# An output product on TensorE: four plain tile products against seven products of half blocks

## The chip, the cores and the metric

The kernel runs on one core of one Trainium2 chip. The metric is the device time of one execution in microseconds (us); where several executions were timed, their median is given.

## The reference, cut to what matters

Two transformer layers run one after the other over 4 sequences of 512 tokens, 512 features wide, all in float32. The first layer adds to its input an attention with 16 heads of 128 features (a sparse part over compressed entries, top 8 of them, and a local window part) and a mixture of experts. The end of that attention is the product in question:

```
merged = (ctx_sparse + ctx_local) * 0.5
out = merged.transpose(0, 2, 1, 3).reshape(Bq, Sq, NH * D) @ Wo + bo
...
x = x + _L0_attn_ref(xn, ...) + _L0_ffn_ref(xn, ...)
```

`merged` has 2048 features (16 heads of 128), and `Wo` takes them to 512. The second layer, an attention with 16 heads of 32 features and another mixture of experts, is not touched.

## The kernel before, in words

Layer 0's attention is cut into 32 steps. A step (index `i`) takes one group `g` of two heads and one sequence `b` of 512 tokens; `b` runs fastest, so that a group's weights serve four steps. Here is what one step does, with the line numbers of the profile:

- `project(i + 1)` makes the queries, keys and values of the *next* step (line 675 records all its matmuls, tile `p`). It already works with seven products of half blocks: `first`, `second`, `third`, `fourth` and `fifth` hold the products p1 to p7, VectorE (DVE) adds their results (lines 710 to 739), and rotates them (lines 585 to 588). `combine_weights` (line 119) makes the sums of weights that it needs, once a group.
- `scores` multiplies this step's queries with compressed keys (`sp`, line 758) and with the window's keys (`st`, line 767). DVE then picks the top 8 of the compressed scores (lines 761 to 783), ScalarE (ACT) takes exponentials (lines 771 and 784), and GpSimd (POOL) multiplies the window's weights with a mask (`lT`, line 775).
- `context` makes the weighted sums of values (lines 809 to 827), for each of the two heads.
- `turn_context` transposes a head's context on TensorE (PE), and ACT copies it to the tile `cT` (lines 834 and 835), which holds [128 features, 2 heads, 512 tokens].
- `output(i, t, cT)`, for the four tiles `t` of 128 tokens, multiplies `cT` with the group's two blocks of `Wo`, adds both heads in one PSUM bank (line 842), and DVE adds the bank to the running sum `acc` (line 845). `acc` holds all 2048 tokens by 512 features in SBUF and becomes the input of the next layer.

PSUM has eight banks: three for the tag `mm` (the products p, `op`, and the experts' products), three for `sc` (scores and contexts), two for `tr` (transposes). A product that wants an `mm` bank waits until DVE has read what stands in it.

Jobs of the rest of the layer are put at fixed places between (`run0((i, place))`): normalising and compressing of sequences in steps 0 to 4, routing in steps 3 and 4, the experts (`hp_r`, line 529, `yr_r`, line 532) from step 5 on, adding their results to `acc` (line 852) from about step 24 on, the first norms of layer 1 in steps 29 to 31. The weights `Wo` of a group are loaded by `load_out` (line 109) into a single buffer at the group's first step, once the last step of the group before has used them. SyncE's queue (SP) issues most transfers; POOL issues the gathers of the experts (lines 481 and 545), whose descriptors go to a scratch in SBUF.

Each engine works through its own queue in order. A scheduler in the framework decides the order in a queue, beginning from the program's order; engines wait for each other by semaphores.

Of the kernel before, what the change touches and what calls it, by code (L numbers as in the profile page):

```python
# [12 lines left out]
F32 = mybir.dt.float32  # L13
I32 = mybir.dt.int32
AF = mybir.ActivationFunctionType
ALU = mybir.AluOpType
# [4 lines left out]
P = 128  # L21
B, S, HID = 4, 512, 512
T = B * S
NT = T // P
TC = S // P
# [24 lines left out]
def two_layers(ctx: ExitStack, tc: tile.TileContext, a: dict, out: bass.AP, large: bass.AP):  # L50
# [3 lines left out]
    nc = tc.nc  # L54
    V, G, A, PE = nc.vector, nc.gpsimd, nc.scalar, nc.tensor
# [8 lines left out]
    wpool = layer0.enter_context(tc.tile_pool(name="wattn", bufs=2))  # L64
    const0 = layer0.enter_context(tc.tile_pool(name="const0", bufs=1))
    qp = layer0.enter_context(tc.tile_pool(name="qkv", bufs=2))
# [6 lines left out]
    def psum(tag, name):  # L73
        return ps.tile([P, 512], F32, tag=tag, name=name, bufs={"mm": 3, "sc": 3, "tr": 2}[tag])

    def load(pool, name, shape, src):
        t = pool.tile(shape, F32, tag=name, name=name, bufs=1)
        nc.sync.dma_start(out=t, in_=src)
        return t
# [8 lines left out]
    def load_block(g, nm, between=None):  # L88


        w = wpool.tile([P, KC, 3 * D], F32, tag=nm, name=f"{nm}_{g}", bufs=1 if nm == "wA" else 2)
        for f in range(2):
            nc.sync.dma_start(out=w[:, ts(f, 2), :],
                              in_=a[nm][g, ts(f, 2 * P), :].rearrange("(k p) c -> p k c", p=P))
            if between:
                between(nm, f)
        return w

    def load_later(g):

        w = load_block(g, "wB")
        b2 = wpool.tile([P, 2, 3 * D], F32, tag="b2", name=f"b2_{g}")
        for i, nm in enumerate(("bA", "bB")):
            nc.sync.dma_start(out=b2[:, i, :], in_=a[nm][g].partition_broadcast(P))
        return [[None, w], b2]

    def load_out(g):
        wo = wpool.tile([P, HG, HID], F32, tag="Wo", name=f"Wo_{g}", bufs=1)
        nc.sync.dma_start(out=wo, in_=a["Wo"][ds(g * HG * D, HG * D), :].rearrange("(h p) c -> p h c", p=P))
        return wo  # L110
# [11 lines left out]
            tc.keep_in_program_order(d)  # L122
        sums_w[g] = t2_, t3_, t4_

    sums_w, out_w = {}, {}
    wk = wv = bkv = cmask = lmask = eidx = row = part = None


    acc = keep.tile([P, NT, HID], F32, tag="acc", name="acc")
# [8 lines left out]
    def load_x(n):  # L138
        nc.sync.dma_start(out=acc[:, n, :], in_=x_v[:, n, :])
# [61 lines left out]
    def tables():  # L201

        for hs, w in ((0, 0), (1, 0), (2, 1)):
            tc.keep_in_program_order(G.tensor_tensor(t1[:, :, hs, :], cos[:, 0:TC], own_(w, TC, 0, R), ALU.mult))
            for half, other in ((0, 1), (1, 0)):
                tc.keep_in_program_order(G.tensor_tensor(t2[:, :, hs, ts(half, 32)], sin[:, 0:TC, ts(half, 32)], own_(w, TC, 32 * other, 32), ALU.mult))
# [252 lines left out]
    class Experts:  # L459
# [53 lines left out]
        def turn(self, i):  # L513
            x = self.x[i]
            tr = self.bank("tr", f"trm_{self.r.name}_{i}")
            for k in range(KC):
                PE.transpose(tr[:, ts(k, P)], x[:, ts(k, P)], ident)  # L517
            xT = self.pool.tile([P, KC, P], F32, tag="xT", name=f"xT_{self.r.name}_{i}")
            A.copy(xT, tr.rearrange("p (k t) -> p k t", k=KC))  # L519
            self.x[i] = xT  # L520
# [117 lines left out]
    steps = [(g, b) for g in range(NH // HG) for b in range(B)]  # L638
# [4 lines left out]
    def load_sums(i):  # L643

        for n in range(4):
            xs[n] = wk0.tile([P, 2, 256], F32, tag=f"x{n}", name=f"x{n}_{i}", bufs=1)
            if i >= B:
                nc.sync.dma_start(out=xs[n].rearrange("p k t -> p (k t)"), in_=xsd[steps[i][1], n])
# [182 lines left out]
    def turn_context(i, h, ctx_, cT):  # L831
        tr = psum("tr", f"trc_{i}_{h}")
        for t in range(TC):
            PE.transpose(tr[:, ts(t, P)], ctx_[:, t, :], ident)
        A.copy(cT[:, h, :], tr)  # L835

    def output(i, t, cT):
        g, b = steps[i]
        wo = out_w[g]
        op = psum("mm", f"op_{g}_{b}_{t}")  # L840
        for h in range(HG):
            PE.matmul(op, lhsT=cT[:, h, ts(t, P)], rhs=wo[:, h, :],  # L842
                      start=(h == 0), stop=(h == HG - 1))
        n = b * TC + t
        V.tensor_tensor(acc[:, n, :], acc[:, n, :], op, ALU.add)  # L845

    def combine(ex, n):
        rs = ex.gather(n)

        def add():  # L850
            for k in range(2):
                tc.keep_in_program_order(V.scalar_tensor_tensor(
                    acc[:, n, :], rs[k], ex.r.gate[:, k, n : n + 1], acc[:, n, :], ALU.mult, ALU.add
                ))
        return add
# [29 lines left out]
    def start_sequence(n):  # L885
        for f in layernorm(n, sp0, psum, n >= TC):
            f()
# [4 lines left out]
    for b in range(1, B):  # L892
        i = b - 2
# [77 lines left out]
    for n in range(3 * TC):  # L971
        i, t = 29 + n // TC, n % TC
        last = t + 2 if t < 3 else 5
        if i + 1 == len(steps) and t == 3:
            last = 4
# [14 lines left out]
    def rest():  # L990
        nonlocal wk, wv, bkv, cmask, lmask, eidx, row, part
        start_sequence(2)
        start_sequence(3)
        tables()
        for n in range(TC, TC + 2):
            load_x(n)
        wk = load(sp0, "wk", [P, KC, D], a["Wk"].rearrange("(k p) d -> p k d", p=P))
        wv = load(sp0, "wv", [P, KC, D], a["Wv"].rearrange("(k p) d -> p k d", p=P))
        bkv = sp0.tile([P, 2, D], F32, tag="bkv", name="bkv", bufs=1)
        nc.sync.dma_start(out=bkv[:, 0, :], in_=a["bk"].partition_broadcast(P))  # L1000
        nc.sync.dma_start(out=bkv[:, 1, :], in_=a["bv"].partition_broadcast(P))
        for n in range(TC + 2, 2 * TC):
            load_x(n)
        out_w[0] = load_out(0)
        cmask = load(const0, "cmask", [P, SEEN[TC - 1].stop], a["c_cmask_seen"])
        lmask = load(const0, "lmask", [P, 2, 2, P], a["c_lmask01"])
        for n in range(2 * TC, NT):
            load_x(n)
        eidx = load(const, "eidx", [P, E], a["c_eidx"])
        row = load(const, "row", [P, P], a["c_row"])  # L1010
        part = load(const, "part", [P, 1], a["c_part"])
# [25 lines left out]
    for i, (g, b) in enumerate(steps):  # L1037
        if b == 0:
            if g:
                out_w[g] = load_out(g)  # L1040
            if g + 1 < NH // HG:
                groups[g + 1] = load_later(g + 1)
        more = i + 1 < len(steps)
        turn_last = turn_keys
        now = qkT
        cT = qp.tile([P, HG, S], F32, tag="cT", name=f"cT_{g}_{b}", bufs=1)
        nc.sync.dma_start(out=cv0s[i % 2][96:P, 0:D], in_=cv[0:32, b, 0:D])
        em0, lT0 = scores(i, 0, now)
        turn_last(1)
        if more:  # L1050
            load_sums(i + 1)
            qkT, sums_x, first, second, third, fourth, fifth, turn_queries, turn_keys = project(i + 1)
            first()
            sums_x()
            if b == 2 and g + 1 in groups:
                groups[g + 1][0][0] = load_block(g + 1, "wA")
        run0((i, 0))
        em1, lT1 = scores(i, 1, now)
        sT0 = turn(i, 0, em0)
        run0((i, 1))  # L1060
        if more:
            second(0)
            turn_queries(0)
        ctx0 = context(i, 0, lT0, sT0, lv)
        if more:
            second(1)
        sT1 = turn(i, 1, em1)
        if more:
            third()
        if b == 2 and g + 1 in groups:  # L1070
            combine_weights(g + 1)
        run0((i, 2))
        ctx1 = context(i, 1, lT1, sT1, lv)
        turn_context(i, 0, ctx0, cT)
        run0((i, 3))
        if more:
            fourth()


            if 5 <= i < 24:  # L1080
                turn_queries(1)
                turn_keys(0)
                fifth()
            else:
                fifth()
        turn_context(i, 1, ctx1, cT)
        if more and not 5 <= i < 24:
            turn_queries(1)
            turn_keys(0)
        run0((i, 3.5))  # L1090
        for t in range(TC):
            output(i, t, cT)
        run0((i, 4))
    scratch.close()
    layer0.close()
# [208 lines left out]
    left = {n: 2 for n in range(NT)}  # L1304
# [159 lines left out]
    for g in range(NG):  # L1464
        b, j = groups1[g]
# [32 lines left out]
    last = [psum1("st", f"o1_{n0 + t}", 2) for t in (0, 2)]  # L1498
    last = [last[t // 2][:, t % 2, :] for t in range(TC)]
# [709 lines left out]
```

## Time and profile before

| what | value |
| --- | --- |
| median of 3 runs | 2061.0 us (2060.38 to 2063.49) |
| profiled execution, its own time | 2062.1 us |
| its span in the profile | 2060.0 us |
| granted TensorE clock | 0.996 |
| PE busy | 2000.5 us, 9130 matmul records |
| DVE busy | 1450.3 us |
| ACT busy | 867.8 us |
| POOL busy | 750.8 us |
| matmuls of line 842 (output) | 512 records of 128x512, 229.0 us |
| adds of line 845 | 128 of 128x512, 87.4 us |

The profile shows each float32 matmul as two records, so that the 8 matmuls of a step's output product stand as 16 records. Durations of matmuls overlap (each is pipelined into the next); the pitch from one to the next is what counts. "Idle before" a group names what its engine waited for. Layer 0's steps lie between about 50 us and 1445 us of the span.

### The profile page before, as it was taken

The numbers are of one execution on the slowest core, as the hardware profiler recorded it, in microseconds if no ns is written. First come the engines' busy times: TensorE is split into PE (matmuls) and PEld (weight loads), VectorE is DVE, ScalarE is ACT, GpSimd is POOL, SyncE is SP. The second block draws the span as 40 slices with busy tenths as digits, with TensorE's granted clock in tenths as the row PEclk, the third lists the DMA queues.
The fourth block names the chain that finished last, engine by engine and source line by source line (L and its number), as shares of the span: only waits on it lengthen the run. The fifth ranks groups of instructions, "written<-read, shape, count | busy, mean of one in ns | idle before, by whom it ended". The sixth has DMA issues, their size and how long they took to land.

```text
span 2060.0 us, 27976 instructions
## 1 busy us (share of the span) xinstructions
PE 2000.5 (97%) x9130; PEld 1199.1 (58%) x9130; DVE 1450.3 (70%) x3543; ACT 867.8 (42%) x2600; POOL 750.8 (36%) x761
## 2 busy tenths in 40 slices
PE   7999999999999999999999999999999999999997
PEld 4666666666666666666666666666334445445442
DVE  7889967666766666676667787787595555557775
ACT  4554444344444443444444454454243432433332
POOL 4422244443323333334334444353114432432550
PEclk9999999999999999999999999999999999999999
DMA  7101133333332343244453222121317775773551
GB/s 251 68 34 60 42 125 133 125 108 113 125 132 101 110 154 103 93 136 162 179 182 113 72 82 75 51 73 62 120 36 260 255 253 200 261 251 119 154 165 51
DMA packets 98906, 267.23 MB, mean 130 GB/s; under 512 B 14400, under 2 KB 27840, under 8 KB 87488
## 3 DMA queue, kind: packets, MB, share of 16 engines
q0 software_dynamic: 27072, 148.91, 21.3%
q1 hardware_dynamic: 70528, 114.34, 16.5%
q10 hardware_dynamic: 1152, 2.10, 0.3%
q8 instruction: 75, 1.23, 0.2%
q14 instruction: 79, 0.65, 0.1%
HBM read 222.05 MB, written 42.73 MB: 129 GB/s over the span
## 4 chain that ended last, share of the span: by engine, by line
PE 80%; DVE 8%; POOL 3%; ACT 3%; issue 2%; DMA 2%; DVEq 0%; ACTq 0%; POOLq 0%
PE p L675 25%; PE hp_r L529 12%; PE op L842 11%; PE st L767 4%; PE sp L758 3%; PE st L1249 2%; PE cx L1263 2%; PE qp L1225 2%; PE ca L811 2%; DVE pS L1269 2%; PE o L1332 1%; PE trq L695 1%; PE trm_r L517 1%; PE trk L701 1%; PE cc L814 1%
## 5 line engine op out<-in xcount | busy, mean ns | idle before, releaser
L842 PE MATMUL op<-Wo,cT 128*128 128x512 f32 x512 | 229.0, 596 | 1.5 <-ACT cT L835 1.1
L529 PE MATMUL hp_r<-we_r,xT_r 128*128 128x512 f32 (+1 forms) x592 | 225.6, 596 | 3.1 <-ACT xT_r L519 2.2
L481 POOL DMA_INDIRECT xr_r<-xnd,rows_r x72 | 88.7, 1232 | 333.5 <-PE trm_r L517 298.6
L775 POOL TENSOR_TENSOR lT<-lT,lmask 128x512 f32<-128x512 f32 (+1 forms) x128 | 155.8, 1229 | 145.9 <-ACT lT L771 145.6
L675 PE MATMUL p<-wT,x 128*128 128x384 f32 x512 | 179.5, 493 | 0.8 <-DVE wT L119 0.8
L675 PE MATMUL p<-wB,x 128*128 128x384 f32 x512 | 176.2, 488 | 2.7 <-DVE u L731 2.6
L675 PE MATMUL p<-wA,xnT 128*128 128x384 f32 x512 | 173.2, 490 | 0.2 <-DVE u L710 0.2
L575 ACT ACTIVATE sq<-qb 128x128 f32<-128x128 f32 x384 | 118.9, 310 | 90.1 <-DVE qb L724 45.2
L842 PEld LDWEIGHTS op<-Wo,cT 128*128 128x128 f32 x512 | 92.3, 190 | 109.3 <-issue 80.9
L1251 ACT ACTIVATE pT<-st 128x1024 f32<-128x1024 f32 x128 | 123.3, 1013 | 62.5 <-PE st L1249 56.8
L529 PEld LDWEIGHTS hp_r<-we_r,xT_r 128*128 128x128 f32 (+1 forms) x592 | 83.2, 170 | 100.0 <-issue 93.4
L845 DVE TENSOR_TENSOR acc<-acc,op 128x512 f32<-128x512 f32 x128 | 87.4, 684 | 70.0 <-PE op L842 69.6
L675 PEld LDWEIGHTS p<-wB,x 128*128 128x128 f32 x512 | 93.7, 190 | 66.8 <-issue 9.6
L675 PEld LDWEIGHTS p<-wT,x 128*128 128x128 f32 x512 | 94.5, 193 | 63.2 <-issue 6.3
L675 PEld LDWEIGHTS p<-wA,xnT 128*128 128x128 f32 x512 | 95.4, 192 | 60.5 <-issue 2.5
L689 ACT ACTIVATE qb<-qb,ss 128x128 f32<-128x128 f32 x256 | 81.9, 390 | 107.5 <-POOL ss L578 104.4
L519 ACT COPY xT_r<-trm_r 128x512 f32<-128x512 f32 x72 | 41.8, 580 | 193.1 <-PE hp_r L529 183.1
L771 ACT ACTIVATE lT<-st,ss 128x256 f32<-128x256 f32 (+1 forms) x128 | 46.8, 447 | 175.4 <-PE st L767 175.4
L767 PE MATMUL st<-qkT 128*128 128x256 f32 (+1 forms) x512 | 108.5, 354 | 1.5 <-ACT qkT L702 1.5
L545 POOL DMA_INDIRECT row_r<-yd,slot_r x64 | 74.4, 1163 | 94.2 <-DVE row_r L1366 36.6
L767 PEld LDWEIGHTS st<-qkT 128*128 128x128 f32 x512 | 92.1, 190 | 11.9 <-ACT qkT L702 1.7
L578 POOL TENSOR_TENSOR ss<-ss,nhalf 128x6 f32<-128x6 f32 x64 | 96.0, 1500 | 5.3
(360 smaller groups left out, 4313.0 us busy)
## 6 DMA issues: line engine op xcount, KB each, us to landing
x<-xsd SPq DMA_DIRECT2D x112, 256.0 KB
yd<-yr_r SPq DMA_DIRECT2D x72, 256.0 KB
wA<-in_wA SPq DMA_DIRECT2D x16, 384.0 KB
wB<-in_wB SPq DMA_DIRECT2D x16, 384.0 KB
xnd<-xn SPq DMA_DIRECT2D x24, 256.0 KB
accd<-acc SPq DMA_DIRECT2D x18, 256.0 KB
acc<-in_x SPq DMA_DIRECT2D x16, 256.0 KB
Wo<-in_Wo SPq DMA_DIRECT2D x8, 512.0 KB
```

The source lines that it names most:

```text
L481: G.indirect_dma_start(out=out, out_offset=None, in_=src, in_offset=at_rows(idx))
L529: PE.matmul(hp[ts(h, m), :], lhsT=xT[:, k, ts(h, m)], rhs=w[:, ts(k, HID)], start=(k == 0), stop=(k == KC - 1))
L545: G.indirect_dma_start(out=x, out_offset=None, in_=self.yd, in_offset=at_rows(self.r.slot[:, k, n : n + 1]))
L575: A.activation(sq, x[:, h, :], AF.Square, accum_out=ss[:, h : h + 1])
L578: pin(G.tensor_tensor(ss, ss, nhalf[:, 0:n], ALU.pow))
L675: PE.matmul(p, lhsT=x[:, k, ts(c, P)], rhs=w[:, k, :], start=(k == 0), stop=(k == 1))
L689: A.activation(x[:, j, :], x[:, j, :], AF.Copy, scale=sq[t][:, j : j + 1])
L767: PE.matmul(st[:, ds((t % 2) * 256, n)], lhsT=qkT[:, HG + h, ts(t, P)], rhs=qkT[:, h, ds(t * P, n)], start=True, stop=True)
L775: G.tensor_tensor(dst, dst, lmask.rearrange("p a w j -> p (a w j)")[:, 0:n], ALU.mult)
L842: PE.matmul(op, lhsT=cT[:, h, ts(t, P)], rhs=wo[:, h, :], start=(h == 0), stop=(h == HG - 1))
L845: V.tensor_tensor(acc[:, n, :], acc[:, n, :], op, ALU.add)
L1251: A.activation(pt[:, ts(pair, 2), :], st, AF.Exp, scale=SCALE1)
```

## The change

A step's output product is the product of `cT` (512 tokens by 256 features, as two halves each way) with the group's `Wo` (256 features by 512). The new `output7` cuts it into 2x2 blocks: a11, a12, a21, a22 are the halves of the tokens (rows) by the two heads, b11 to b22 the two heads by the halves of the 512 columns. Seven products of such blocks (256 tokens by 128 features by 256 columns) replace eight. Sums of blocks are made for it on DVE:

- `combine_out(g)` makes three sums of `Wo`'s blocks (tile `WoT`) and overwrites b12, four instructions of 128x256, once a group.
- `rest()` makes s1, s2, s4 (tile `cS`) and overwrites a21, four instructions of 128x256 in each step.

Results go to four banks, x, y, z and w. The first product of x is added to a part of `acc`, then a second product is accumulated on it in the same bank and the sum is added to another part, then a third, which is added to both halves of the columns at once; z is read twice in that way. `before()` stands ahead of the transpose of the second head, as its product needs the first head alone. The scratch for the descriptors of POOL's transfers is set to 8192 bytes of each partition, half of the default, and the two new tiles take 3072 bytes of each partition apiece.

```
+    def combine_out(g):
+        wo = out_w[g]
+        b11, b12, b21, b22 = (wo[:, h, c] for h in range(2) for c in (low, high))
+        t = wpool.tile([P, 3, 256], F32, tag="WoT", name=f"WoT_{g}", bufs=1)
+        V.tensor_tensor(t[:, 0, :], b12, b11, ALU.subtract)
+        V.tensor_tensor(b12, b22, b12, ALU.subtract)
+        V.tensor_tensor(t[:, 1, :], b22, t[:, 0, :], ALU.subtract)
+        V.tensor_tensor(t[:, 2, :], t[:, 1, :], b21, ALU.subtract)
+        out_t[g] = t
+
+    def output7(i, cT):
...
+        def product(x, left, right, last=True):
+            new = x not in banks
+            if new:
+                banks[x] = psum("mm", f"o{x}_{g}_{b}")
+            p = banks[x]
+            for c in range(2):
+                PE.matmul(p[:, ts(c, 256)], lhsT=left[:, ts(c, P)], rhs=right, start=new and c == 0, stop=True,
+                          skip_group_check=True)
+
+        def add(x, half, cols, op=ALU.add):
+            p = banks[x].rearrange("p (c f) -> p c f", c=2)
+            own = acc[:, ds(b * TC + 2 * half, 2), :]
+            if cols is None:
+                own = own.rearrange("p c (f x) -> p c f x", f=2)
+                p = p.unsqueeze(2).to_broadcast([P, 2, 2, 256])
+            else:
+                own = own[:, :, cols]
+            V.tensor_tensor(own, own, p, op)
+
+        def before():
+            product("x", a11, wo[:, 0, low], False)
+            add("x", 0, low)
+
+        def rest():
+            s = qp.tile([P, 3, 256], F32, tag="cS", name=f"cS_{g}_{b}", bufs=1)
+            s1, s2, s4 = (s[:, n, :] for n in range(3))
+            product("y", a12, wo[:, 1, low])
+            V.tensor_tensor(s1, a21, a22, ALU.add)
+            V.tensor_tensor(s2, s1, a11, ALU.subtract)
+            product("w", a22, wt[:, 2, :])
+            add("y", 0, low)
+            V.tensor_tensor(a21, a11, a21, ALU.subtract)
+            product("x", s2, wt[:, 1, :], False)
+            V.tensor_tensor(s4, a12, s2, ALU.subtract)
+            add("x", 0, high)
+            product("z", s1, wt[:, 0, :], False)
+            add("w", 1, low, ALU.subtract)
+            product("x", a21, wo[:, 0, high])
+            add("z", 1, high)
+            product("z", s4, wo[:, 1, high])
+            add("x", 1, None)
+            add("z", 0, high)
+        return before, rest
...
+        if b == 0:
+            combine_out(g)
...
+        before, rest_ = output7(i, cT)
+        before()
         turn_context(i, 1, ctx1, cT)
...
-        for t in range(TC):
-            output(i, t, cT)
+        rest_()
...
-    nc = _bacc.Bacc("TRN2", target_bir_lowering=False, num_devices=1)
+    nc = _bacc.Bacc("TRN2", target_bir_lowering=False, num_devices=1, dynamic_dma_scratch_size=8192)
```

More of the change, by code (lines that the diff above doesn't have):

```diff
@@ L123, in combine_weights @@
         sums_w[g] = t2_, t3_, t4_
-    sums_w, out_w = {}, {}
+    sums_w, out_w, out_t = {}, {}, {}
     wk = wv = bkv = cmask = lmask = eidx = row = part = None
@@ L845, in output @@
         V.tensor_tensor(acc[:, n, :], acc[:, n, :], op, ALU.add)
+    low, high = slice(0, 256), slice(256, HID)
+    def combine_out(g):
[7 more added lines that the diff above has]
+        out_t[g] = t
@@ new lines, in output7 @@
+    def output7(i, cT):
+        g, b = steps[i]
+        wo, wt = out_w[g], out_t[g]
+        a11, a21, a12, a22 = (cT[:, h, c] for h in range(2) for c in (low, high))
+        banks = {}
+        def product(x, left, right, last=True):
[38 more added lines that the diff above has]
+        return before, rest
```

## The prediction

> **What bounds the kernel now.** I read the page first: how busy each engine is over the span.
>
> ```profile
> PE 2000.5 (97%) x9130; PEld 1199.1 (58%) x9130; DVE 1450.3 (70%) x3543; ACT 867.8 (42%) x2600; POOL 750.8 (36%) x761
> PE   7999999999999999999999999999999999999997
> DVE  7889967666766666676667787787595555557775
> ```
>
> PE is the bound, but DVE is at eight or nine tenths in the first slices. So I asked for busy times by stretch (columns: stretch, its length, then PE, PEld, DVE, ACT, POOL), for three stages of layer 0.
>
> ```profile
> 140.00:190.00 50.00, 48.65 (x236) 32.26 (x235) 42.55 (x118) 22.61 (x80) 12.59 (x16) 1.00 0.22 69
> 190.00:240.00 50.00, 47.87 (x225) 32.23 (x224) 45.96 (x179) 22.40 (x80) 12.60 (x12) 1.00 0.11 33
> 560.00:605.00 45.00, 45.00 (x201) 29.56 (x200) 29.02 (x76) 19.99 (x70) 14.07 (x15) 1.00 0.33 114
> 1190.00:1235.00 45.00, 45.00 (x216) 30.94 (x215) 36.18 (x106) 22.92 (x80) 22.55 (x21) 1.00 0.28 83
> ```
>
> Three stages, then. **Early**, steps 0 to 4 (45 us each): DVE 85 to 92% busy. **Steady**, steps 5 to 23: PE without a gap, DVE 65%. **Late**, steps 24 to 31 (some 39 us each): DVE 80%. Next the chain of waits, around the end of a steady step (start, length, what; x counts records).
>
> ```profile
> 403.63 6.95 PE op L842 x16
> 410.58 0.89 PE sp L758 x8
> 411.47 1.52 PE st L767 x8
> 412.99 0.44 PE trk L701 x4
> ```
>
> All of it is PE: what is taken out there shortens the step, unless DVE takes its place. How near DVE is, its own order of instructions shows, around the end of another steady step (start, length), and after it the groups by form.
>
> ```profile
> 588.90 0.68 DVE L845 TENSOR_TENSOR acc<-acc,op 128x512 f32<-128x512 f32 x1
> 590.36 0.69 DVE L845 TENSOR_TENSOR acc<-acc,op 128x512 f32<-128x512 f32 x1 [0.78 <-PE op L842]
> 592.08 0.69 DVE L845 TENSOR_TENSOR acc<-acc,op 128x512 f32<-128x512 f32 x1 [1.03 <-PE op L842]
> 593.79 0.69 DVE L845 TENSOR_TENSOR acc<-acc,op 128x512 f32<-128x512 f32 x1 [1.03 <-PE op L842]
> ...
> 596.83 1.18 DVE L782 TENSOR_TENSOR rep<-s,rep 128x320 f32<-128x320 f32 x1
> 598.05 1.17 DVE L783 SCALAR_TENSOR_TENSOR s<-rep,s 128x320 f32<-128x320 f32 x1
> 599.14 0.55 DVE L710 TENSOR_TENSOR u<-p,b 128x384 f32<-128x384 f32 x1
> ...
> 607.65 0.49 DVE L783 SCALAR_TENSOR_TENSOR s<-rep,s 128x320 f32<-128x320 f32 x1
> ```
>
> ```profile
> L845 DVE TENSOR_TENSOR acc<-acc,op 128x512 f32<-128x512 f32 x128 | 87.4, 684 | 70.0 <-PE op L842 69.6
> L1269 DVE TENSOR_TENSOR pS<-pS,pT 128x1024 f32<-128x1024 f32 x64 | 77.2, 1233 | 3.9 <-ACT pT L1251 3.7 <-issue 0.2
> ```
>
> DVE rests between the output's adds, and from the last of them to line 710 it never rests. Line 710 matters: it empties the bank of the next projection's first product, and with three banks its fourth product waits for that.
>
> **The change, part by part.** *PE.* A step's output is 16 records in 6.95 us, 0.434 each. It becomes 7 products x 2 column blocks x 2 records = 28 records of 256 columns. Price of one: `st` takes 1.52 us for six records of 256 and two of 128, and one of 128 takes 0.11 (`trk`, 0.44 for 4), so (1.52 - 0.22) / 6 = 0.217, just half of 0.434. 28 x 0.217 = 6.07, a saving of 0.88 us a step, 28 us in 32 steps.
>
> [...] The rows of 128, 256, 384 and 512 columns here (0.11, 0.217, 0.322, 0.434 each) lie on a line through nothing; I go by them.
>
> *DVE.* A step loses four adds and gets six of the same 512 elements, one of 1024 and four sums of 128x256. The adds cost 0.68 (line 845); the wide one about 1.2 (line 1269, the nearest row; its operands lie in SBUF, here one is PSUM read twice); a sum 0.34, the time from one 128x256 instruction of line 585 to the next start (586.93 to 587.27). Added: 2 x 0.68 + 1.2 + 4 x 0.34 = 3.9 us a step, 125 us in all. `combine_out` adds 4 x 0.34 = 1.4 for each of 8 groups. What covers this is DVE's rest just there: the idle time before lines 845, 588 (of `lv`, where it waits for ACT) and 761. By stage: steady 51.8 + 15.2 + 3.8 = 70.8 us in 19 steps, 3.7 a step; early 7.2 + 0 + 3.7 in 5, 2.2 a step; late 11.0 + 2.0 + 2.3 in 8, 1.9 a step.
>
> *Steady.* In the step shown PE reached the fourth product at 600.24 (first at 596.37, three of 1.29 between). Its bank was free at 599.69 (599.14 + 0.55), and PE starts 0.05 after such a release (a wait that ended at 195.40 after a line 710 that ended at 195.35): 0.5 us to spare. Now PE would be there at 599.36, and line 710 ends 3.9 - 3.7 = 0.2 later, 599.89: the product starts at 599.94, a gain of 0.3. Bounds: lines 782 and 783 took 1.18 and 1.17 while POOL multiplied masks (596.39 to 598.86), and line 783 took 0.49 at 607.65 with POOL at rest. If the new order frees them, line 710 comes up to 1.4 earlier and the gain is the whole 0.88. If the new sums are held instead (a 128x256 instruction of line 588 took 1.28 at 138.20 for 0.43 elsewhere, 0.85 more), the step loses 0.5. I take a gain of 0.45, between the paced value and the middle of the upper part: 19 x 0.45 = -8.6 us.
>
> The waits inside the seven products I take at nothing: between a product and the next one on its bank PE has another product of 0.87 us, and DVE's add takes 0.6 to 0.7. It costs 0.2 a step and more if DVE comes late to them.
>
> *Early.* 3.9 - 2.2 = 1.7 us without cover, less the 0.5 that PE had to spare: 1.2 lost a step. Bounds: nothing, if the 7.0 us that DVE waits for ACT before line 827 take it up, and 3.9, where DVE has no rest at all. That is step 3 with the routing (45.96 of 50): I take 3.0 there. 4 x 1.2 + 3.0 = +7.8.
>
> *Late.* 3.9 - 1.9 = 2.0 without cover. In the changed program line 710 stands ahead of both lines 782 and 783 in six of the seven late steps that have it, before in two; in most that takes one of them, 0.49 at rest and 1.18 beside a mask, out of its way. So the loss is 2.0 less 0.5 (PE's spare time) and less 0.5 to 1.2: 0.3 to 1.0. I take 0.6. Bounds: a gain of 0.88 and a loss of 2.0. 8 x 0.6 = +4.8.
>
> *The rest.* `combine_out` stands between lines 710 and 711 on DVE; the queries made there are transposed at 610.72 while POOL's step for them ended at 606.01, so I cost it nothing (1.4 x 8 = 11 us without that cover). It reads `Wo` 6 us or more after the load's issue, which landed in some 3.3 us (593.72 to 597.0), and SP has nothing queued behind that it holds up. At the end of layer 0 the first rows of `acc` are complete only after the last two adds, not after the first: +1 (0 to 3). The halved scratch: POOL's gathers moved 27072 packets in 268 transfers, and no wait shows a full scratch; nothing, and POOL's longest idle time is waiting for PE anyhow.
>
> Sum: -8.6 + 7.8 + 4.8 + 1 = +5 on the profiled execution's 2062.1, so 2067.1; the median of the runs lies 1.1 below it: 2066. A measurement tells about 0.2%, 4.1 us, from no change.
>
> **Rivals.** *Not slower: the masks let go of DVE* (0.33). The new order puts part of `st` ahead of the output's products, so POOL's masks come earlier, beside adds that read PSUM. [...] For it: line 717, which reads PSUM, kept 0.55 at 1230.37 within a mask. [...] It decides where line 710 comes at least 0.6 us earlier after the projection's last product than the 13.0 us of before (586.13 to 599.14). Then steady gains 16.7, late gives and takes nothing, early costs 5, the end 1: 2061.0 - 10.7, about 2050.
>
> *DVE becomes the bound outside the steady steps* (0.13): three of the sums held by 0.85 in 13 steps, 33 us, and steady gains 8.6 as above: about 2085. For it, 92% in the second stretch.
>
> *All covered* (0.04): 2061 - 28 = 2033; against it, the late and early rests are below 3.9. *Narrow products are no cheaper* (0.04): by the group's busy time a record of 256 is 94.4 / 384 = 0.246 us, 28 make 6.9, the saving is gone: about 2085.
>
> **How the numbers follow.** My own case has 0.46, with 2059 to 2075 for itself: steady between 0 and 0.7 a step. The range 2046 to 2084 leaves out the two outer cases and the ends of the others, about 0.2. Faster by over 0.2% (below 2056.9): most of the first rival and the covered case, 0.31. Within: the rest of that rival and the lower part of mine, 0.22. Slower: 0.47.
>
> **What would show it.** Right: about 6.1 us of PE for a step's products; DVE busy near 1590; steady steps 0.3 to 0.6 shorter, with PE's waits on line 710 and on the adds; steps 0 to 4 longer, step 3 most; late steps slightly longer. Wrong: PE waits inside the seven products of over 0.5 a step, 256-column records beyond 0.23, or late steps that gain.

## The result, and the profile after

| | before | changed |
| --- | --- | --- |
| median, 20 runs each | 2060.9 us (2059.0 to 2063.9) | 2062.2 us (2059.5 to 2068.3) |
| profiled execution, its span | 2062.1, 2060.0 us | 2060.0, 2058.2 us |
| PE busy | 2000.5 us | 1982.5 us |
| DVE busy | 1450.3 us | 1545.9 us |

The ratio of the times is 1.0006 (95% interval 0.9999 to 1.0013): no difference that can be told, within the range that was forecast (2046 to 2084, most likely 2066). Three terms behind it were far off, and cancelled. From the page of the changed kernel, the busy line and DVE's share in 40 slices:

```profile
PE 1982.5 (96%) x9514; PEld 1276.0 (62%) x9514; DVE 1545.9 (75%) x3799; ACT 864.3 (42%) x2600; POOL 745.4 (36%) x761
DVE  7889987777776777786678888887696555557675
```

The chain of waits around the output of a steady step (start, length, what):

```profile
591.59 0.86 PE ox L873 x4
592.45 0.44 PE trc L834 x4
592.89 0.89 PE sp L758 x8
593.78 0.43 PE st L767 x2
594.22 0.86 PE oy L873 x4
...
599.83 0.65 PE st L767 x4
```

Four records of 256 columns take 0.86, 0.216 each, half of the 0.434 of a wide one: seven products take 6.05 us for 6.95. The chain is still all PE. The scheduler put the next step's scores (`sp`, `st`) between the products, as cover. DVE's and POOL's instructions at the end of the same step:

```profile
599.05 1.27 POOL L775 TENSOR_TENSOR lT<-lT,lmask 128x512 f32<-128x512 f32 x1 [3.44 <-ACT lT L771]
599.06 1.21 DVE L884 TENSOR_TENSOR acc<-acc,ox 128x1024 f32<-128x1024 f32 x1
600.19 0.68 DVE L884 TENSOR_TENSOR acc<-acc,oz 128x512 f32<-128x512 f32 x1
...
601.33 1.00 POOL L775 TENSOR_TENSOR lT<-lT,lmask 128x384 f32<-128x384 f32 x1 [1.00 <-ACT lT L771]
...
601.72 0.95 DVE L782 TENSOR_TENSOR rep<-s,rep 128x320 f32<-128x320 f32 x1
602.71 0.49 DVE L783 SCALAR_TENSOR_TENSOR s<-rep,s 128x320 f32<-128x320 f32 x1
603.12 0.55 DVE L710 TENSOR_TENSOR u<-p,b 128x384 f32<-128x384 f32 x1
```

Line 710 starts 11.7 us after the projection's last product (591.43), before 13.0; PE has 0.95 us to spare at the product that waits for it (in most steady steps; 0.54 before). The first mask ran beside an add that reads PSUM, and that add took the 1.21 that all 32 of its kind take. Lines 782 and 783 have both inputs in SBUF. Where a mask ran beside it, line 782 took 1.11 us on average, and 0.49 with POOL at rest (1.20 and 0.49 before); line 783 took 0.87 and 0.49 (1.01 and 0.48 before). Over the whole span of the changed kernel:

```profile
L782 DVE TENSOR_TENSOR rep<-s,rep 128x320 f32<-128x320 f32 x64 | 64.3, 1004 | 1.4
L783 DVE SCALAR_TENSOR_TENSOR s<-rep,s 128x320 f32<-128x320 f32 x64 | 42.9, 670 | 1.4
```

They had means of 1158 and 918 ns. The 25.7 us that they lost are one reason why DVE's busy time rose by 96 us and not by the 140 of the forecast (1590).

To see where time went I cut layer 0 of both traces into steps, at the starts of one product that each step has once (line 675, `p<-wT,xnT`), and took the difference of each step to the kernel before. Steps that an edit does not touch agree within 0.02 us between kernels, a few within 0.25.

| step | 0 | 1 | 2 | 3 | 4 | 5 | 6 to 21, each | 22, 23 | 24 | 25 | 26 | 27 | 28, 29 |
| --- | --- | --- | --- | --- | --- | --- | --- | --- | --- | --- | --- | --- | --- |
| changed - before, us | +4.2 | +2.5 | +1.7 | +2.6 | +0.1 | -0.5 | -0.90 | -1.1, -1.1 | +1.2 | +1.1 | +3.3 | +1.9 | -0.2, -0.2 |

Steps 0 to 3 lose 10.9 us, steps 4 to 23 gain 17.1, steps 24 to 29 lose 7.2, the rest of layer 0 0.3: +1.3, as the medians say. (The two profiled executions differ the other way, by what comes before and after these steps: layer 1, where nothing was edited, took between 608.8 and 613.3 us in the traces of this study.)

### The profile page after: what moved, and what is told of

It reads as the page before. It is cut to its first block, busy times and chain, and to the rows that moved or that the text cites. A ratio compares the mean times of both kernels' runs of the same rounds, so it can differ in the third digit from the quotient of the medians.

```text
span 2058.2 us, 28987 instructions
## 1 busy us (share of the span) xinstructions
PE 1982.5 (96%) x9514; PEld 1276.0 (62%) x9514; DVE 1545.9 (75%) x3799; ACT 864.3 (42%) x2600; POOL 745.4 (36%) x761
## 4 chain that ended last, share of the span: by engine, by line
PE 73%; DVE 12%; ACT 4%; POOL 3%; issue 2%; DMA 1%; ACTq 0%; DVEq 0%; SPq 0%; POOLq 0%
PE p L675 21%; PE hp_r L529 12%; PE st L767 4%; PE ox L873 3%; PE st L1316 2%; PE oz L873 2%; PE qp L1292 2%; PE sp L758 2%; PE cx L1330 2%; DVE pS L1336 2%; PE ca L811 2%; PE o L1399 1%; PE trm_r L517 1%; ACT sq L575 1%; PE vp L1252 1%
## 5 line engine op out<-in xcount | busy, mean ns | idle before, releaser
L767 PE MATMUL st<-qkT 128*128 128x256 f32 (+1 forms) x512 | 116.0, 354 | 1.3 <-ACT qkT L702 1.3
L577 POOL TENSOR_SCALAR ss<-ss 128x6 f32<-128x6 f32 x64 | 31.1, 486 | 163.1 <-ACT sq L575 162.7
L675 PE MATMUL p<-wT,xnT 128*128 128x384 f32 x256 | 88.0, 487 | 0.0
L884 DVE TENSOR_TENSOR acc<-acc,ox 128x512 f32<-128x512 f32 (+1 forms) x96 | 82.3, 857 | 5.0 <-PE ox L873 4.4
```

What stands on the lines that cost most here:

```text
L675: PE.matmul(p, lhsT=x[:, k, ts(c, P)], rhs=w[:, k, :], start=(k == 0), stop=(k == 1))
L767: PE.matmul(st[:, ds((t % 2) * 256, n)], lhsT=qkT[:, HG + h, ts(t, P)], rhs=qkT[:, h, ds(t * P, n)], start=True, stop=True)
L884: V.tensor_tensor(own, own, p, op)
```

## The experiments

What each run lost or gained against the kernel before, by steps, in us. The last column names the steps from 0 to 29 that hold a stretch in which the granted clock, the share of its full speed that TensorE was given, stood at 0.50. Runs c1 to c7 are one execution each.

| run | steps 0 to 2 | step 3 | 4 to 23 | 24 to 27 | half clock in step (us) |
| --- | --- | --- | --- | --- | --- |
| the change | +8.4 | +2.6 | -17.1 | +7.5 | 2 (3.41), 3 (3.41) |
| s1_steady | 0 | 0 | -17.5 | 0 | none |
| s2_first | +7.7 | +3.1 | +0.4 | -0.2 | 3 (3.41) |
| s3_last | +0.2 | 0 | +0.6 | +7.6 | none |
| c1_no_sums | +6.6 | +4.5 | -18.6 | +5.0 | 3 (6.83) |
| c2_first_with_rest | +5.7 | +1.5 | -16.9 | +9.4 | 26 (3.41) |
| c3_pool_sums | +6.6 | +4.4 | -18.2 | +5.4 | 3 (3.41) |
| c4_more_sums | +8.4 | +1.5 | -14.6 | +8.7 | 2 (3.41), 26 (3.41) |
| c5_turn_first | +6.1 | +1.5 | -17.4 | +2.8 | none |
| c6_many_sums | +7.7 | +2.8 | +12.2 | +6.5 | 3, 5, 23 (3.41 each) |
| c7_x_in_sc | +8.1 | +5.0 | -16.8 | +7.3 | 3 (6.83), 25 (3.41) |
| d1_plain_more_dve | -1.1 | +4.7 | +0.4 | +7.6 | 3 (3.41) |

The last column matters for every reading of steps 0 to 3. Each of these stretches begins during a wait of PE of 1.7 to 4.2 us or within 1.2 us after it; not each such wait brings one (the 2.84 us of step 26 did in c2 and c4, not in the change). In the kernel before there is none in these steps. What one costs, step 3 of the change and then of c4_more_sums tells, which has the same edit there and the same waits (columns as in the prediction, then granted clock, DMA share, GB/s):

```profile
217.10:262.63 45.53, 41.52 (x215) 31.02 (x214) 41.88 (x147) 19.14 (x67) 10.31 (x10) 0.96 0.12 36
216.13:260.56 44.43, 40.39 (x214) 29.83 (x213) 41.76 (x146) 18.79 (x66) 10.29 (x10) 1.00 0.14 37
```

That is 1.1 us; in step 2 it is 0.7 (+1.7 in the change and c4, +1.0 in s2 and c6). So some 1.8 of the change's 10.9 us in steps 0 to 3 are the lower clock that followed PE's waits, and at full clock it would lose 9.1 there.

**The change taken apart.** The seven products in some groups only, the plain four tiles in the others:

```
+        seven = 1 <= g <= 5          # s2_first: g == 0; s3_last: g >= 6
-        if b == 0:
+        if b == 0 and seven:
             combine_out(g)
...
+        if seven:
             rest_()
+        else:
+            for t in range(TC):
+                output(i, t, cT)
```

> Seven products only in groups 1 to 5 (steps 4 to 23), the plain four tiles in groups 0, 6 and 7. Theory A, read from the two traces step by step: a steady step gains 0.90 us whatever happens before and after, and nothing of that hangs on the other groups: 18 x 0.90 + 1.1 less 0.1 in step 4 = 17 us, so about 2044 (2042 to 2047). Theory B, the terms of the prediction: 0.45 a step, 8.6 us, about 2052. Theory C: what the first steps lose is only pushed to later steps (the experts' jobs start when routing is done), and the steady gain is partly that being made up: 2047 to 2056.

Measured: 2040.9 us beside 2062.2, ratio 0.991 (0.989 to 0.992), a little below A's 2042 to 2047. Of the 24.4 us between the two traces, 17.5 lie in steps 4 to 23, as A has it, and 4.5 in layer 1, which the edit does not touch. The steady gain stands by itself; B's 2052 falls.

> Seven products only in group 0 (steps 0 to 3). Theory A: these four steps lose 4.2 + 2.5 + 1.7 + 2.6 = 11.0 us in the trace, and nothing makes it up later: about 2072 (2069 to 2075). Theory B (prediction): 4 x 1.2 and the routing's step 3.0, +7.8: 2069. Theory C (made up later): 2061 to 2065.

Measured: 2070.1 us, ratio 1.005 (1.003 to 1.006); steps 0 to 3 lose 10.8 and nothing makes it up. A; the time alone would not exclude B's 2069, the steps do.

What PE loses in steps 0 to 2 has several parts. One is no wait: the eight records of the router's logits (line 263) took 1.00 us together before, and the output's products now stand between the second and the third. Step 0 before, then two rows of the changed kernel:

```profile
97.88 1.07 PE L263 MATMUL lg_r<-xnT,wr 128*32 128x512 f32 x8
```

```profile
97.51 1.04 PE L263 MATMUL lg_r<-xnT,wr 128*32 128x512 f32 x2
...
100.41 1.06 PE L263 MATMUL lg_r<-xnT,wr 128*32 128x512 f32 x6
```

The two take 0.98 us and the six 0.99. The same happens in step 1, and in both steps of every run with seven products there; where the plain product stands, in d1 too, they take 1.00. That makes 2.0 of the 8.4 us. The others are waits, 7.5 us in steps 0 to 2 against 2.5 before (length of a step less PE's busy time), some of them new in the changed kernel:

```profile
PE trck L631 <- ACT ck L628: 2.0, 2, 1.2
PE ox L873 <- DVE cS L895: 1.9, 1, 1.9
```

With the 0.7 us of the clock and less the 2.7 that PE saves, 5.0 of the 8.4 us are accounted for; the other 3.4 are not.

> Seven products only in groups 6 and 7 (steps 24 to 31). Theory A: the trace loses 1.2 + 1.1 + 3.3 + 1.9 in steps 24 to 27 and gains 0.2 in steps 28 and 29: +7.2, about 2068 (2066 to 2070). Theory B (prediction): +4.8 and +1 at the layer's end, 2067. The two lie too close to tell by the time; the trace tells: by A PE waits for ACT (the copies of cT, the queries of line 689), by B for DVE (line 710 or the adds).

Measured: 2069.8 us, ratio 1.004 (1.003 to 1.005). PE's waits in steps 24 to 27 (for whom, us in all, times, longest; the largest of ten):

```profile
PE trq L695 <- ACT qb L689: 3.4, 3, 2.9
PE trk L701 <- ACT cT L835: 3.2, 3, 1.1
PE ox L873 <- DVE u L731: 0.9, 2, 0.5
```

As A has it, PE waits for ACT more than for DVE.

The halved scratch alone (one argument of the program's constructor):

> The kernel before with the scratch of dynamic transfers halved and nothing else. Prediction and theory A: no change, 2061 (2059 to 2063). Rival: POOL's gathers wait for room in the scratch and the experts' jobs come later: 2064 or more, with POOL's gathers of lines 481 and 545 longer than before.

Measured: 2061.2 beside 2062.2 us, ratio 0.9994 (0.9985 to 1.0004); its steps are those of before within 0.25 us, and POOL's gathers of line 481 take 1234 ns for 1232. It costs nothing.

**Is it DVE's work?** The four sums left out:

```
-            V.tensor_tensor(s1, a21, a22, ALU.add)
-            V.tensor_tensor(s2, s1, a11, ALU.subtract)
...
-            V.tensor_tensor(a21, a11, a21, ALU.subtract)
-            V.tensor_tensor(s4, a12, s2, ALU.subtract)
+            s1, s2, s4 = a21, a11, a12
```

> The changed kernel without the four sums that DVE makes of cT in a step (the products read blocks of cT as they are, so the output is not the reference's); the three sums of Wo stay. 1.4 us of DVE less in each step. Theory D (DVE is the bound where a step loses): steps 0 to 3 get back up to 1.4 each, 5.5 of their 11.0, and steps 24 to 27 as much, 5.5 of their 7.5; steady steps stay. Theory O (the loss is the order of work on PE, ACT and POOL: PE stands before a transpose that waits for a copy of ACT, with nothing left to cover it): steps 24 to 27 stay within 1 us of 7.5, and steps 0 to 3 get back only what PE waited for line 895 and the adds in front of a product, about 2 to 3. My guess: D for steps 0 to 3, O for steps 24 to 27.

Measured: steps 0 to 3 lose 11.1 with as much time at half clock as the change, nothing is got back, and my guess for them was wrong. Steps 24, 25 and 27 keep their losses (+1.4, +1.2, +2.4); step 26 went from +3.3 to 0, so that steps 24 to 27 lose 5.0, less than O's 7.5 within 1. The reason is POOL's queue. POOL in step 26 of the changed kernel, and then without the sums:

```profile
1263.38 2.86 POOL L775 TENSOR_TENSOR lT<-lT,lmask 128x512 f32<-128x512 f32 x2 [2.81 <-ACT lT L771]
1266.32 0.52 POOL L577 TENSOR_SCALAR ss<-ss 128x6 f32<-128x6 f32 x1
```

```profile
1261.49 0.43 POOL L577 TENSOR_SCALAR ss<-ss 128x6 f32<-128x6 f32 x1 [3.60 <-ACT sq L575]
1262.00 1.75 POOL L578 TENSOR_TENSOR ss<-ss,nhalf 128x6 f32<-128x6 f32 x1
1263.74 2.57 POOL L775 TENSOR_TENSOR lT<-lT,lmask 128x512 f32<-128x512 f32 x2
```

With the sums, the scheduler put two masks ahead of the queries' norm, and PE waits 2.84 us for the queries. Before, the norm came first, as it does here.

The four sums on POOL (`G` in place of `V` in groups 0, 6 and 7):

> The changed kernel with the four sums of cT on POOL in groups 0, 6 and 7. Theory D: DVE is 1.4 us a step lighter there, so steps 0 to 3 lose 5 to 6 less than 11.0, as without the sums. Against it: each sum waits for the one before and POOL does 128x512 masks in 1.2 us, so a sum may take 0.6 or more, and the chain of three comes 1 us later to the products, and the masks hold DVE. If PE waits for the chain, steps 0 to 3 lose 11 or more and steps 24 to 27 more than 7.5. My guess: steps 0 to 3 lose 8, steps 24 to 27 lose 8.

Measured: steps 0 to 3 lose 11.0 (PE now waits 1.5 us for an add in step 0), step 26 0.1, steps 24 to 27 5.4. DVE's lighter load gives nothing back in steps 0 to 3; the guess of 8 was wrong both times.

**Is it the place of the products?** The first product together with the other six:

```
-        before()
+        if not (i < 4 or i >= 24):
+            before()
         turn_context(i, 1, ctx1, cT)
...
+        if (i < 4 or i >= 24):
+            before()
         rest_()
```

> The changed kernel, but in steps 0 to 3 and 24 to 31 the first of the seven products is issued together with the other six, behind the transposes of the second head's context and of the next queries, where the plain product stood. All work of DVE is kept. Theory O: PE's waits of 1.0 to 1.1 for ACT's copy of cT (line 835) and of 0.45 for line 731 in steps 24, 25, 27 and 28 go; steps 24 and 25 go from +1.15 each to between -0.9 and -0.3, step 27 from +1.9 to +0.5 or less; step 26 keeps its 2.84 of waiting for the queries (POOL's masks stay ahead of the norm there), +1.5 to +2.5. Theory D: steps 24 to 27 stay at +7.5 within 1.5, since DVE has the same work. Steps 0 to 3: D says 11.0 within 1.5; O says less than 7.

Measured: steps 0 to 3 lose 7.2, 3.7 less, of which 1.8 is the clock, at 1.00 here; what the edit took away is 0.8 in step 0 and 1.2 in step 1. Steps 24 and 25 only went from +1.2 and +1.1 to +0.8 each, and step 27 rose to +3.0: O's numbers fail there. (Step 26, +4.9, has the same wait of 2.84 as in the change, and half clock behind it.) The waits named went, and others came. PE's waits in steps 24 to 27:

```profile
PE trq L695 <- ACT qb L689: 4.7, 3, 2.8
PE oy L873 <- DVE lv L739: 2.1, 3, 0.7
PE ox L873 <- DVE cS L895: 1.4, 3, 0.5
```

PE now came to the second product before DVE had emptied the projection's bank (line 739), and to the fourth before its sum was made. So I tried the order of the steady steps, which puts scores in between:

```
-            if 5 <= i < 24:
+            if True:
                 turn_queries(1)
                 turn_keys(0)
                 fifth()
...
-        if more and not 5 <= i < 24:
+        if False:
             turn_queries(1)
```

> The changed kernel with the order of steps 5 to 23 in all steps: the last transposes of the next queries and keys go ahead of the projection's fifth product, so that scores of the next step can stand between that product and the output's seven. Theory O (the loss outside steps 5 to 23 is that PE comes to the seven products before DVE has emptied the projection's banks and made the sums, with no scores to put between): the waits of lines 834/701 for line 835 and of the output's products for lines 731, 739 and 895 go, and steps 24, 25 and 27 get down from +1.2, +1.1 and +1.9 to between -0.9 and 0, unless PE now waits for the queries (line 695 for line 689) ahead of the fifth product, which costs 1 to 3 a step. Theory D (DVE's work): steps 24 to 27 stay at +7.5 within 1.5. Steps 0 to 3: by O 11 gets to 4 or less, by D it stays.

Measured: 2052.5 us in one execution, beside 2061.4 in one of the kernel before; steps 24 to 27 +0.9, +0.7, +0.4 and +0.8 in place of +1.2, +1.1, +3.3 and +1.9, steps 0 to 3 7.5, at full clock (the change there 9.1). Better, but none of these steps came near the -0.9 that PE saves. PE's waits in steps 24 to 27:

```profile
PE oy L873 <- ACT cT L835: 2.3, 3, 0.9
PE trq L695 <- ACT qb L689: 2.0, 1, 2.0
```

A bank more for the products, taken from the scores (`psum("sc" if x == "x" and not 1 <= g <= 5 else "mm", ...)`):

> The changed kernel with the bank that three of the seven products share (ox) taken from the three banks of scores and contexts instead of the three of products, in groups 0, 6 and 7. Theory O with banks as its cause: the waits of ox for line 731 and of oy for line 739 go (0.45 to 0.7 a step), and one of those inside the products (0.2 to 0.7), so steps 24, 25, 27 and steps 0 to 3 lose 0.5 to 1 less each, unless scores wait for the bank instead. Theory D: no change by more than 0.3 a step.

Measured: steps 0 to 3 lose 13.1, steps 24 to 27 7.3 (a stretch at half clock in step 25 is in it). The waits for lines 731 and 739 went, and PE waited 6.2 us for the copies of `cT` in place of 3.9. The banks alone are not the cause.

**How much can DVE take?** In steps 5 to 23, four and then twelve sums more:

```
             add("z", 0, high)
+            if 5 <= i < 24:
+                for _ in range(4):        # c6_many_sums: 12
+                    V.tensor_tensor(s2, s1, a11, ALU.subtract)
```

> The changed kernel with one of the four sums (s2) made four times more behind the last product that reads it, in steps 5 to 23: 1.4 us more of DVE in a steady step (the same values are written again). By the prediction's way of counting (the order of DVE's instructions is kept): line 710 ends 0.95 us before PE's fourth product in the changed kernel, so a step gets 1.36 - 0.95 = 0.4 longer, 45.3, +7 us in all. Theory A: the scheduler puts line 710 ahead of lines 782 and 783 when DVE has more to do; that gives back 1.0 to 1.5, and a steady step stays at 44.87.

Measured: 44.87 in most steady steps, as A says; line 710 stands ahead of lines 782 and 783 in each and in most ends 0.63 us before it is needed. Steps 5 and 23, at the edges of the edit, lose 0.4 and 1.6 more, which makes most of the 2.5 between the two rows of the table.

> As the run with four more sums in a step, but twelve more (4.1 us of DVE in steps 5 to 23). With four more, line 710 moved ahead of line 782 and ended 0.63 before PE needed its bank. Eight more are 2.7 us; with nothing left to move, a step gets 2.1 longer: about 47.0 instead of 44.87, some 38 us in all. If the scheduler can put the added sums behind line 710 too, a step stays below 45.5.

Measured: 45.8 in most, neither of the two: 4.1 us more of DVE made a step 0.92 longer. The scheduler put part of the sums behind line 710. (Steps 5 and 23, with half clock, lose 3.5 and 6.2 more than in the changed kernel, and are left aside.) PE's waits between 360 and 900 us, of which the changed kernel shows none:

```profile
PE p L675 <- DVE u L710: 9.2, 12, 1.3
```

**The plain product with the added work of DVE.** The reverse test, on the kernel before:

```
         for t in range(TC):
             output(i, t, cT)
+            for n in range(3):
+                V.tensor_tensor(s[:, n, :], cT[:, 0, 0:256], cT[:, 1, 0:256], ALU.add)
```

> The kernel before (plain four tiles, halved scratch) with twelve sums of 128x256 more on DVE in each step, three behind each tile's add, written to a tile that nothing reads: 4.1 us more of DVE a step, as much as the seven products add (3.9), while PE keeps the plain product. Theory D (DVE's added work is what steps 0 to 3 and 24 to 27 lose by): they lose what they lost in the changed kernel, 11.0 and 7.5, less the 0.9 a step that PE does not save here, or more exactly 12 to 15 and 9 to 11; steady steps, where the added work was covered, stay at 45.78; in all 2084 or more. Theory O (the loss is in the seven products' own waits: PE stands for banks, sums and copies between and ahead of them): steps 0 to 3 lose 5 or less, steps 24 to 27 3 or less, steady steps nothing, in all 2062 to 2070.

Measured: 2074.6 us, ratio 1.006 (1.004 to 1.007), between the two. Steps 0, 1 and 2: 0.0, 0.0, -1.1. Step 3: +4.7. Steps 24 to 27: +1.8, +1.8, +2.2, +1.8. PE's waits in steps 24 to 27, the first:

```profile
PE p L675 <- DVE u L710: 5.8, 4, 1.6
```

O is right for steps 0 to 2: twelve sums, 4.0 us in each step, cost nothing there, though DVE is 85 to 96% busy. (Its busy time rose by 2.0 to 2.6 us a step, since other instructions got shorter; in the change it rose by 3.0 to 5.0, so the test is a little lighter than the change.) In step 3 the work costs 3.0 us or more: PE waits 3.15 for the queries in place of 1.2, and of the 4.7 at most 1.7, half of 3.41, is the clock. Steps 24 to 27 lose 7.6, nearer to D's 9 to 11 than to O's 3: this work alone costs as much as the change did. But in the changed kernel PE does not wait for line 710 there; it stands earlier in the step, for ACT's copies. One wait seems to have taken the other's place: that would explain why taking DVE's sums away (c1, c3) gave nothing in steps 24, 25 and 27, and why moving the products (c2) brought waits for DVE out again. No run tests this by itself.

## Why the prediction was right, point by point

The time was right, within 4 us, by luck: errors of 8.5 us on one side and 5.5 on the other that cancelled.

- *PE's saving, 0.88 a step.* Right: 0.90. The price from the row of `st` held (0.216 for 0.217). The 28 records of 256 columns take 6.05 us in a steady step, where the 16 wide ones took 6.95.
- *Steady, -8.6.* The direction was right, the size half: -17.1. The step that failed is the value of 0.45 taken between the bounds 0.88 and -0.5; the upper bound was it. I had summed DVE's added work against its rest at one place and kept the order of its instructions. Four more sums cost nothing and eight more on top of them 0.92: beyond the 3.9 us of the change, by an estimate some 3.2 us of DVE's time were still free in a step (4.1 - 0.92). Line 710 was the right place to look at; it came 1.3 us earlier, not 0.2 later.
- *The first rival's condition* (line 710 at least 0.6 earlier) came true, and its steady 16.7 too. Its 2050 did not, since early steps cost 10.9 for its 5 and late ones 7.2 for its 0. Adds that read PSUM kept their time beside masks: 17 of the 32 adds of 1024 in the changed kernel ran beside one and took 1.21 us each, and those with POOL at rest 1.22. Instructions with two SBUF inputs took longer there (line 782 1.11 us on average for 0.49; in c4 the added sums took 642 ns on average, 411 with POOL at rest and 1051 beside a mask). No run here took the masks away, so how much of the 1.3 us is theirs was not measured by itself.
- *Early, +7.8.* +10.9 in steps 0 to 3, and the mechanism fails in three of the four: "1.7 us without cover, less the 0.5 that PE had to spare" was DVE's arithmetic, and with the plain product that much of DVE's work costs nothing in steps 0 to 2. What stands there is the router's logits cut in two (2.0), waits and the clock (0.7). Only step 3, taken at 3.0, shows DVE's work costing time by itself (2.6 in the change, 1.1 of it the clock; at least 3.0 with the plain product). The prediction had no term for the clock.
- *Late, +4.8.* +7.2 to step 29. DVE's price was counted right: 2.0 without cover less 0.5 is 1.5, and with the plain product PE waited 1.5 to 1.6 for line 710 in three of those steps. But the changed kernel shows other waits: 1.0 to 1.1 for the copy of `cT`, 0.45 for line 731, and 2.84 once behind POOL's masks, which the prediction did not have. (Before, line 710 stands ahead of both lines in one late step, not in two.)
- *The waits inside and ahead of the seven products*, taken at nothing: right in steps 5 to 22, where PE has none; 0.15 to 2.0 us a step in steps 0 to 3 and 0.4 to 0.7 in steps 24 to 27. That is the sign of being wrong that the prediction named, over 0.5 a step, in steps 0, 2, 3 and 26.
- *The rest.* The scratch costs nothing, and `combine_out` nothing in steps 8, 12, 16 and 20, which gain 0.90 like the others; the layer's end costs 0.3.

What is settled is where the change gains and loses, what the loss in step 26 is (POOL's order), that the logits cut in two and the clock are 2.7 of the 8.4 us of steps 0 to 2, and that DVE's amount of work does not by itself make the rest. Which waits make the rest stays open: each rearrangement took 0.3 to 2.7 us of the 8.4 away, the clock's 0.7 included, and none most of it. PE stands there by turns for adds, sums, ACT's copy of `ck` (line 628) and banks.

The version to keep is s1_steady, seven products in groups 1 to 5: 2040.9 us, 1% below both kernels.

## What to carry to other kernels

As I read these runs, a plain product that needs nobody for 7 us is also the cover under which other engines catch up; a cheaper one that leans on DVE every 0.86 us takes that cover away. It paid where the next step's scores stood between its parts (steps 5 to 23) and not elsewhere, though putting them there in all steps (c5) brought only part of it back; so try it stage by stage. When the total does not move, cut the trace into steps before believing that nothing happened: here -17 and +18 lay under +1. Look at the granted clock of each step before putting a microsecond down to an edit. The scheduler moved instructions here when the load changed (in c4 line 710 stands ahead of lines 782 and 783), so rest summed at one place was less than DVE could still take, and the group of the router's logits was cut in two.

## What the runs showed that I had not expected

- An engine 85 to 92% busy was not on the path: in d1, 4.0 us more of DVE's sums a step left steps 0 and 1 the same to 0.01 us.
- Some waits of PE cost twice here: behind some of those of 1.7 us and more the granted clock stood at 0.50 for 3.41 or 6.83 us, 0.7 to 1.2 us more where two like steps can be compared.
- Eight records of 32 weight columns by 512 took 1.00 us together; with other products between, two took 0.98 and six 0.99.
- The masks' hold on DVE moves with the order of work: line 782 took 1158 ns on average before, 1004 in the changed kernel, 872 with four more sums, 612 with twelve.
